# A two-layer graph network with experts: GpSimd adds half of the six expert answers to the other half, and TensorE sums the rest with 12 transposes, not 24

## The chip, the cores and the metric

The kernel runs on one core of a Trainium2 chip. The core has five engines that work side by side, each through its own list of instructions, in order: TensorE (PE in the profile, its weight loads PEld), VectorE (DVE), ScalarE (ACT), GpSimd (POOL) and SyncE (SP), which here only issues DMA transfers. TensorE writes to PSUM; the others work on SBUF, and VectorE and ScalarE read PSUM too. The metric is the device time of one execution in microseconds. Of three runs of the kernel before, the median is 2058.91 us (2055.96 to 2059.22).

## The reference

The input is 8192 tokens of 256 numbers (128 graphs of 64 nodes). There are two layers, each a graph step and an expert step. The part around the change is the end of layer 0 and the start of layer 1:

```python
# layer 0, experts: top 6 of 64, each a 256x256 matrix
xW = einsum('bsd,bskde->bske', x, lattice_weights[indices])   # six answers a token
lattice_out = einsum('bske,bsk->bse', xW, scores)             # their weighted sum
h = x + einsum('bsd,ed->bse', lattice_out, out_w) + out_b
x = x_in + layer_norm(h)                                      # x_in: the input of this step
# layer 1, graph step
h = layer_norm(x)
conv = (adj @ h) @ W_rel + b_rel + h @ W_root
x = x + relu(conv)
```

Then layer 1 routes every token to its top 2 of 8 experts with a hidden layer of 512 and adds their two answers. All of it is float32.

## The kernel before

The work is cut into 32 blocks of 256 tokens (two tiles of 128, `T = 2`). It runs in four stages. The first does layer 0's graph step and sends each token six times to a table in DRAM that is sorted by expert. The second walks that table in pages of 128 rows, multiplies each page by its expert's matrix, scales the rows by the token's score and scatters them to `r0.answer` in DRAM, so that the six answers of a token lie side by side. The third, called the fused pass here, is the one that the change touches. The fourth does layer 1's experts, again page by page.

The fused pass takes a block through these steps:

- `load_y` (L970) brings the block's answers into the tile `y`, 128 partitions x 2 tiles x 6 answers x 256 numbers, with two DMAs of 768 KB. For the first five blocks (`READY = 5`) it need not wait for the last answers, for the later ones it must.
- `load3` (L979) loads `xn1`, `x1` and the adjacency.
- `mixture` (L987) both sums the six answers and turns them: for each half of the 256 numbers and each tile, six matmuls with the identity, marked as transposes, are accumulated in PSUM (L994). That is 24 a block. ScalarE copies the result to `accT` (L997).
- `out_proj` (L999) is the product with `out_w`; `layer_out_h`, `_a`, `_b`, `_c` (L1008 to L1049) are the residual and both layer norms, mostly on VectorE (L1011, L1017, L1026, L1028 and the statistics of L45 and L46).
- `flip_h`, `neighbours`, `convolve_a`, `convolve_b` (L1051 to L1084) are layer 1's graph step on TensorE, and `residual1_a`, `residual1_b` (L1086, L1094) its residual and norm.
- `flip3` and `gate1` (L1102, L1108) compute the routing logits on TensorE; `choose1` (L1115) starts on VectorE with L1118, finds the two experts, and has GpSimd write the token numbers into `xs` (`compare`, L292); `count1` counts on TensorE (L217).
- `place1` and `send1` (L1129, L1136) work out each token's row on VectorE (L313 to L327, then L296) and send it with an indirect DMA from GpSimd (L334), four a block. `xs` has three buffers.

The loop is software-pipelined. `staggered` (L486) runs through steps; in step s, a stage with lag g works on block s - g. So `load_y` with lag -3 works three blocks ahead of `layer_out_h` with lag 0, and `mixture` with lag -2 two blocks ahead. Within a step the order is that of the list at L1143.

The order of instructions on TensorE, VectorE and ScalarE is this written order (`manual_schedule`, L515). On GpSimd and SyncE a planner sets the order at compile time: it plays the program through with estimated costs and takes, on each of these engines, what it believes to be ready first. On GpSimd, for instance, the `compare` of a block stands ahead of the last sends of the block before. Every engine then works through its list strictly in order; waits between engines and on DMAs are semaphores that the framework places. A tile name with `bufs=n` has n buffers in turn; the work pool of this pass gives two where nothing else is said, so `y` has two, and the load of a block's `y` waits for the `mixture` of two blocks before.

Of the kernel before, what the change touches and what calls it, by code (L numbers as in the profile page):

```python
# [9 lines left out]
F32 = mybir.dt.float32  # L10
# [6 lines left out]
ALU = mybir.AluOpType  # L17
AX = mybir.AxisListType
PSUM = bass.MemoryType.PSUM
P = 128  # L20
# [465 lines left out]
def staggered(n, stages, first=0):  # L486

    for s in range(first + min(lag for lag, _ in stages), n + max(lag for lag, _ in stages)):
        for lag, f in stages:
            if first <= s - lag < n:  # L490
                f(s - lag)
# [3 lines left out]
def two_layer_gnn_moe_kernel(ctx: ExitStack, tc: tile.TileContext, a: dict, out: bass.AP):  # L495
    nc = tc.nc
    x_in, adjT = a["x"], a["adjT"]
    N, D = x_in.shape
# [4 lines left out]
    T = 2  # L503
# [5 lines left out]
    K0 = 6  # L509
    E1, F1, _ = a["L1_ffn_W2"].shape  # L510
    EARLY = 12
    READY = 5
# [91 lines left out]
    with tc.tile_pool(name="c0", bufs=1) as c0, \  # L604
# [9 lines left out]
        blocks = [dict() for _ in range(NB)]  # L614
# [213 lines left out]
        n = free[0] // 16  # L828
# [118 lines left out]
    with tc.tile_pool(name="c3", bufs=1, reuse_waits="tile") as c3, \  # L947
# [17 lines left out]
        blocks = [dict() for _ in range(NB)]  # L965
# [3 lines left out]

        def load_y(b):  # L970
            B = blocks[b]
            B["y"] = y = work.tile([P, T, K0, D], F32, name="y")
            for t in range(T):
                d = nc.sync.dma_start(out=y[:, t],
                                      in_=r0.answer[ts(b * T + t, P * K0), :].rearrange("(p k) d -> p k d", k=K0))
                if b < READY:
                    tc.declare_no_dep(d.ins, group="r0last", reason="in the first pages, or waited for above")

        def load3(b):  # L979
            B = blocks[b]  # L980
            B["xn1"] = xn1 = work.tile([P, T, D], F32, name="xn1", bufs=3)
            nc.sync.dma_start(out=xn1, in_=by_tile(xn1_dram[b]))
            B["x1"] = x1 = work.tile([P, T, D], F32, name="x1", bufs=3)
            nc.sync.dma_start(out=x1, in_=by_tile(x1_dram[b]))
            B["at"] = load_adjacency(b)

        def mixture(b):  # L987

            B = blocks[b]
            pt = psum.tile([P, KD, C], F32, name="ps")  # L990
            for t in range(T):
                for k in range(KD):
                    for i in range(K0):
                        nc.tensor.matmul(pt[:, k, ts(t, P)], lhsT=B["y"][:, t, i, ts(k, P)], rhs=ident,  # L994
                                         start=(i == 0), stop=(i == K0 - 1), is_transpose=True)
            B["accT"] = accT = work.tile([P, KD, C], F32, name="accT")
            nc.scalar.copy(accT, pt)  # L997

# [137 lines left out]
        def send1(b, i):  # L1136
# [4 lines left out]
            r1.send(B["row"], B["xs"], b > NB // 2, (k,), (t,))  # L1141

        staggered(NB, (  # L1143
            (-3, load_y),
            (-2, load3),
            (0, layer_out_h),
            (3, choose1),
            (-2, mixture),
            (1, flip_h),
            (3, count1),  # L1150
            (2, residual1_a),
# [127 lines left out]
```

## Time and profile before

| what | value |
|---|---|
| median of three runs | 2058.91 us |
| the profiled execution, its own time | 2052.92 us |
| its span, first to last instruction | 2051.1 us |
| mean granted TensorE clock | 0.974 |
| busy: TensorE / its weight loads | 1923.0 us (94%) / 1678.1 us (82%) |
| busy: VectorE / ScalarE / GpSimd | 1200.0 (59%) / 1018.1 (50%) / 1162.0 us (57%) |
| the fused pass, about | 1131 to 1525 us of the span |
| L994, the transposes of the answers | 768, 94.7 us of TensorE busy |

The profile is one execution. Engine times are the union of its instructions' times, so an engine at 94% over the whole span can be full in one stage and wait in another; the shares must be read by stage. Rows of a timeline give the start, the length, the engine, the line of the kernel, the operation, what it writes and reads with their shapes, and in brackets how long the engine had stood idle before it and what ended that. Rows of a single line or tile give the shortest, median and longest duration in ns. The time of an indirect DMA on GpSimd is that of its issue, not of the transfer.

### The profile page before, as it was taken

To read this page: it belongs to the slowest core of one execution; us is meant where nothing else is said; L and a number is where in the kernel's file an instruction comes from. 1 tells how busy PE (TensorE), PEld (TensorE's weight loads), DVE (VectorE), ACT (ScalarE), POOL (GpSimd) and SP (SyncE) were. 2 spreads that over 40 slices of the span, in tenths; PEclk is the share of its full clock that TensorE was granted. 3 is DMA by queue.
4 is the path that set the end of the run, shared out by engine and by line. 5 is a ranking of instruction groups with operands and counts; after the bars stand their busy time and mean duration, and the time that the engine had idled before them with its cause. 6 is when DMAs were issued, how large, how long until landed. Compare 5 with 4: busy or idle time off the path is not lost. (4 is left out here: it accounts for less than half of the span.)

```text
span 2051.1 us, 37214 instructions
## 1 busy us (share of the span) xinstructions
PE 1923.0 (94%) x10516; PEld 1678.1 (82%) x10516; DVE 1200.0 (59%) x4205; ACT 1018.1 (50%) x2033; POOL 1162.0 (57%) x1134
## 2 busy tenths in 40 slices
PE   6999999999966989999999799999989999999996
PEld 5888888888865778888877688888868888888885
DVE  5899999999975333344333389999862222222221
ACT  4888888888851222222222266666643333333332
POOL 1377667677677777777777723333343444444443
PEclk9999999999977999999999899999989999999998
DMA  4244555544476988666665799888527766666664
GB/s 123 80 143 148 168 165 170 169 159 141 133 267 206 309 252 267 214 207 207 207 207 171 266 362 338 267 278 278 190 92 172 178 162 162 162 163 163 163 163 86
DMA packets 282561, 397.91 MB, mean 194 GB/s; under 512 B 56025, under 2 KB 236393, under 8 KB 282353
## 3 DMA queue, kind: packets, MB, share of 16 engines
q1 hardware_dynamic: 202880, 246.61, 40.2%
q0 software_dynamic: 64416, 136.14, 22.1%
q10 hardware_dynamic: 15056, 12.69, 1.9%
q8 instruction: 94, 1.54, 0.3%
q14 instruction: 115, 0.93, 0.2%
HBM read 222.84 MB, written 176.64 MB: 195 GB/s over the span
## 5 line engine op out<-in xcount | busy, mean ns | idle before, releaser
L334 POOL DMA_INDIRECT r0x<-xs,r0row x384 | 402.1, 1047 | 236.0 <-DVE lat L706 72.2
L341 POOL DMA_INDIRECT r0y<-px x404 | 393.3, 973 | 123.3 <-DMA r0y<-px 49.7
L918 PE MATMUL py<-lat,pxT 128*128 x1616 | 389.4, 384 | 18.7 <-ACT pxT L905 15.4
L351 POOL DMA_INDIRECT out_x<-py_s,px x138 | 214.6, 1555 | 293.8 <-DMA out_x<-py_s,px 125.9
L922 DVE TENSOR_SCALAR px<-py,px 128x256 f32<-128x256 f32 x404 | 177.0, 480 | 309.6 <-PE py L918 303.9
L918 PEld LDWEIGHTS py<-lat,pxT 128*128 128x128 f32 x1616 | 294.3, 192 | 59.3 <-ACT pxT L905 20.4
L905 ACT COPY pxT<-pt 128x512 f32<-128x512 f32 x202 | 117.9, 585 | 368.6 <-PE pt L903 252.7
L1217 ACT ACTIVATE phid<-ph,pw 128x256 f32<-128x256 f32 x276 | 130.6, 473 | 323.2 <-issue 213.9
L1215 PE MATMUL ph<-pxT,pw 128*128 128x256 f32 x1104 | 251.3, 381 | 0.7 <-ACT pxT L1206 0.7
L1235 PE MATMUL py<-fw,phid 128*128 (+1 forms) x1104 | 249.7, 379 | 0.0
L717 PE MATMUL ps<-lat 128*128 128x256 f32 x1024 | 238.5, 382 | 0.0
L1215 PEld LDWEIGHTS ph<-pxT,pw 128*128 128x128 f32 x1104 | 210.9, 191 | 30.0 <-ACT pxT L1206 1.1
L684 PE MATMUL ph<-lat 128*128 128x256 f32 x1024 | 232.2, 386 | 2.7 <-DVE lat L706 2.0
L1235 PEld LDWEIGHTS py<-fw,phid 128*128 128x128 f32 x1104 | 204.5, 190 | 25.0
L684 PEld LDWEIGHTS ph<-lat 128*128 128x128 f32 x1024 | 195.1, 193 | 29.4 <-issue 2.4
L334 POOL DMA_INDIRECT r1x<-xs,r1row x128 | 127.7, 998 | 160.9 <-DVE r1run L313 47.0
L717 PEld LDWEIGHTS ps<-lat 128*128 128x128 f32 x1024 | 193.8, 192 | 24.9
L1229 DVE TENSOR_SCALAR p<-p 128x2 f32<-128x2 f32 x69 | 12.8, 186 | 225.5 <-ACT p L1228 225.5
L1238 DVE TENSOR_TENSOR py_s<-py,pb 128x512 f32<-128x512 f32 x69 | 47.7, 692 | 154.9 <-PE py L1235 152.7
L903 PE MATMUL pt<-ident,px 128*128 128x128 f32 x808 | 125.3, 276 | 11.6 <-DMA px<-r0x 11.3
L903 PEld LDWEIGHTS pt<-ident,px 128*128 128x128 f32 x808 | 100.4, 142 | 37.7 <-DMA px<-r0x 8.9
L994 PE MATMUL ps<-ident,y 128*128 128x128 f32 x768 | 94.7, 281 | 16.1 <-DMA y<-r0y 16.1
(303 smaller groups left out, 2980.4 us busy)
## 6 DMA issues: line engine op xcount, KB each, us to landing
px<-r0x SPq DMA_DIRECT2D x404, 129.0 KB
y<-r0y SPq DMA_DIRECT2D x64, 768.0 KB
pw<-in_L_ffn_W1b SPq DMA_DIRECT2D x69, 514.0 KB
px<-r1x SPq DMA_DIRECT2D x69, 258.0 KB
x<-x SPq DMA_DIRECT2D x64, 256.0 KB
pb<-in_L_ffn_b SPq DMA_DIRECT2D x69, 128.0 KB
r0x<-r0filler ACTq DMA_DIRECT2D x64, 129.0 KB
lat<-in_x SPq DMA_DIRECT2D x32, 256.0 KB
```

The costliest lines, as they stand in the source:

```text
L334: i = self.nc.gpsimd.indirect_dma_start(out=self.table[:, :], out_offset=bass.IndirectOffsetOnAxis(ap=row[:, t, k:k + 1], axis=0), in_=xs[ ...
L341: d = self.nc.gpsimd.indirect_dma_start(out=self.answer[:, :], out_offset=bass.IndirectOffsetOnAxis(ap=x[:, self.D:self.D + 1].bitcast(I32 ...
L351: i, d = f"{self.name}add{i}", self.nc.gpsimd.indirect_dma_start(out=self.total[:, :], out_offset=bass.IndirectOffsetOnAxis(ap=x[:, self.D ...
L684: nc.tensor.matmul(ph[:, c, :], lhsT=w1[:, k, ts(2 * j + c, P)], rhs=B["aggT"][:, k, :], start=(k == 0), stop=(k == KD - 1))
L717: nc.tensor.matmul(B["po"][:, t, :], lhsT=B["hT"][:, c, ts(t, P)], rhs=w2[:, c, :], start=False, stop=(t == T - 1 and c == KH - 1))
L903: nc.tensor.transpose(pt[:, k, ts(q, P)], Q["px"][:, q, ts(k, P)], ident)
L905: nc.scalar.copy(xT[:, :, :n * P], pt[:, :, :n * P])
L918: nc.tensor.matmul(py[:, q, :], lhsT=xT[:, k, ts(q, P)], rhs=lat[:, ds(regs["e"][(2 * j + q) % 4], 1), k, :].rearrange("p o d -> p (o d)") ...
L922: nc.vector.tensor_scalar(px[:, q, :D], py[:, q, :], px[:, q, D + 1:D + 2], None, op0=ALU.mult)
L1215: nc.tensor.matmul(ph, lhsT=w[:, k * F1 + c * P:k * F1 + (c + 1) * P], rhs=Q["xT"][:, k, :], start=(k == 0), stop=(k == KD - 1))
L1217: nc.scalar.activation(hid[:, c, :], ph, AF.Relu, bias=w[:, KD * F1 + c:KD * F1 + c + 1], scale=1.0)
L1235: nc.tensor.matmul(py[:, t, :], lhsT=Q["hid"][:, c, ts(t, P)], rhs=fw2[:, ds(e, 1), c, :].rearrange("p o d -> p (o d)"), start=(c == 0), s ...
```

## The change

From block 6 on (`b > READY`), a new step `halve` has GpSimd add the last three answers of each token to the first three, in place in `y`: two adds a block, each 128 partitions x 768 float32. `mixture` then accumulates three transposes for each quarter, 12 a block. The first six blocks are summed as before, by 24. `halve` works three blocks ahead (lag -3, listed behind `mixture` of the block before it), so `load_y` moves from three to four blocks ahead, and `y` gets a third buffer: 12,288 bytes more in each partition of the pass's work pool.

```diff
         def load_y(b):
             B = blocks[b]
-            B["y"] = y = work.tile([P, T, K0, D], F32, name="y")
+            B["y"] = y = work.tile([P, T, K0, D], F32, name="y", bufs=3)
...
+        def halve(b):
+
+            B = blocks[b]
+            B["n"] = K0
+            if b > READY:
+                B["n"] = h = K0 // 2
+                y = B["y"]
+                for t in range(T):
+                    nc.gpsimd.tensor_tensor(y[:, t, :h], y[:, t, :h], y[:, t, h:], op=ALU.add)
...
             for t in range(T):
                 for k in range(KD):
-                    for i in range(K0):
+                    for i in range(B["n"]):
                         nc.tensor.matmul(pt[:, k, ts(t, P)], lhsT=B["y"][:, t, i, ts(k, P)], rhs=ident,
-                                         start=(i == 0), stop=(i == K0 - 1), is_transpose=True)
+                                         start=(i == 0), stop=(i == B["n"] - 1), is_transpose=True)
...
         staggered(NB, (
-            (-3, load_y),
+            (-4, load_y),
             (-2, load3),
             (0, layer_out_h),
             (3, choose1),
             (-2, mixture),
+            (-3, halve),
             (1, flip_h),
```

## The prediction

> **What bounds the kernel now.** I read the chain of waits first, cut to the fused pass (1131 to 1525 us of the span), because the change touches only that pass. Columns: start, us, what.
>
> ```profile
> 1305.31 0.92 PE pg L1112 x8
> 1306.23 2.67 PE ps L994 x24
> 1308.90 0.44 PE ps L76 x4
> ...
> 1316.35 0.92 PE pg L1112 x8
> 1317.28 2.67 PE ps L994 x24
> ```
>
> One block takes 1317.28 - 1306.23 = 11.05 us and the chain never leaves TensorE: the pass looks TensorE-bound, and the 24 transposes of L994 are 2.67 us of each block, 0.111 us apiece. Second, the busy time by stretch, one steady block and then one block after the last transposes of L994 were done (1474.9 us), so a block in which TensorE has none of them left.
>
> ```profile
> core 0: us, PE busy (x) PEld busy (x) DVE busy (x) ACT busy (x) POOL busy (x), PEclk, DMA share, GB/s
> 1305.05:1316.10 11.05, 11.05 (x76) 9.90 (x74) 10.03 (x47) 7.15 (x17) 4.17 (x5) 1.00 0.78 244
> 1483.30:1494.00 10.70, 8.95 (x51) 7.28 (x50) 9.89 (x46) 6.17 (x14) 3.82 (x6) 1.00 0.21 74
> ```
>
> TensorE is full in the first and VectorE is at 10.03 of 11.05. In the second TensorE is down to 8.95 us, and VectorE's work is what it was. Third, then, VectorE's timeline: the instruction that opens each block's routing (L1118), three blocks in a row.
>
> ```profile
> 1472.25 0.17 DVE L1118 TENSOR_TENSOR logits<-pg,r_L_ffn_bg 128x16 f32<-128x16 f32 x1 [0.23 <-PE pg L1112]
> ...
> 1483.29 0.17 DVE L1118 TENSOR_TENSOR logits<-pg,r_L_ffn_bg 128x16 f32<-128x16 f32 x1 [0.23 <-PE pg L1112]
> ...
> 1494.03 0.16 DVE L1118 TENSOR_TENSOR logits<-pg,r_L_ffn_bg 128x16 f32<-128x16 f32 x1
> ```
>
> With the transposes a block took 11.04 us, of which VectorE waited 0.23 for TensorE. Without all 24 of them it took 10.74, and VectorE waited for nothing. So 10.74 us is VectorE's own time for a block, and TensorE hides a second bound only 0.31 us below its own. This is the view that decides the case.
>
> Fourth, whether GpSimd and VectorE disturb each other. Two pairs, from the timeline and from the instructions of one tile:
>
> ```profile
> 1156.78 0.66 DVE L1017 TENSOR_TENSOR x<-x,r_L_ffn_ln_b 128x512 f32<-128x512 f32 x1
> 1156.87 1.41 POOL L341 DMA_INDIRECT r0y<-px  x1 [0.30 <-DMA r0y<-px]
> ```
> ```profile
> L334 POOL DMA_INDIRECT r1x<-xs,r1row x128: 958/970/1524, 1194.4 to 1531.3; - x128
> L327 DVE CAST r1row<-r1rowf x32: 169/382/391, 1193.3 to 1524.6; 128x4 int32<-128x4 f32 x32
> ```
>
> A Pool instruction that takes 0.97 us took 1.41 when a VectorE instruction with two inputs in SBUF was running: 0.44 more. In the other direction the small CAST of L327 takes 0.17 us alone and 0.38 beside a Pool DMA issue: at 1304.36 it ended at 1304.74, with the issue of 1303.80 (0.97 us). They do make each other wait, in both directions.
>
> **The change, part by part.** *TensorE.* 26 blocks (6 to 31) lose 12 transposes each: 12 x 0.111 = 1.33 us of a block, 34.7 us in all, if TensorE alone set the pace. It does not: the block falls from 11.05 to 10.74 and stops there, because VectorE is next. That is worth 0.31 us a block.
>
> *Pool.* 52 adds of 128x768 f32, two a block. No row shows such an add. Low end: Pool's fills, from 128x1 in 99 ns to 128x516 in 528, cost 0.83 ns an element, so 0.74 us. One pass that reads and writes is the AFFINE_SELECT, 128x128 in 282 ns: (282 - 99) / 128 = 1.43 ns an element, so 0.1 + 1.1 = 1.2 us. High end: that pass twice, 2.3 us. I take 1.8, the read-and-write pass plus a second read at the fills' pace (0.64), as the add reads two operands and writes one. [...] Pool itself has room: 4.17 us busy in a block, 7.8 with the adds.
>
> *What the adds do to VectorE.* This is the term that decides. About a third of VectorE's instructions in a block read two tiles in SBUF (L209, L296, L68, L1017, L1026, L1028, L323, L1042), and the two casts behave as L327 does. No row shows an add on Pool beside them. From both sides: nothing is lost (the DMA issues, which read only an index, leave L323 at its 0.19), or such an instruction waits until the add is over, as the cast waited for the issue. I take the second, because the add streams SBUF through all of its time and the cast's row, where Pool also keeps moving data, is the nearest. I laid two adds of 1.8 us into the block from 1305.37 to 1316.40. Example, behind the token-number instruction that ends at 1309.05: the first add ends at 1310.85, L296 waits for it from 1309.41 (1.44 us); the second runs from 1310.98 to 1312.78, and L1017, now due at 1311.98, waits 0.80; together 2.24. Behind each of the four sends it is 3.49, 2.21, 3.44, 2.79; over all starting points of the block 2.7, which I take, as the planner's place for the adds is not known. With 0.74 us the mean is 0.8, with 2.3 it is 3.7 and the worst place 4.5. A block then takes 10.74 + 2.7 = 13.44 us, 2.39 more than now. Of 26 blocks I count 25 (the first pair falls into the wait for the last answers, before 1186 us): +60 us. [...]
>
> *The wait that is added.* A block's transposes now wait for its two adds; behind them on TensorE stand flip_h, the counts and all the rest of the block. The adds are due a whole block earlier, so I cost it at nothing; the cover is one block (13 us). On Pool an add waits for its y tile; behind it stand the compare and four sends, which free xs (three buffers).
>
> *y one block earlier, a third buffer.* The same 64 loads. SP issues each right after the transposes three blocks before (0.8 to 1.5 us of SP time, as now); 0.78 of the DMA engines' time is used in a steady block, so nothing. At the start block 5's y waits for the last answers (issued 1179.65) and now stands before block 3's xn and x loads (1159.21, 1162.02 now). VectorE's L1011 of block 3, at 1181.32 now, may slip until that y has landed, 1185.86: 0 to 4.6 us. I take 2. Below nothing: block 6's y gets out some 3 us sooner, but TensorE waits for no y after 1185.86.
>
> **Sum.** +60 + 2 = +62 us. On the profiled execution (span 2051.1, time 2052.9) that makes 2114.9; the median of the three runs, 2058.9, lies 6.0 above it, and I forecast against the median: 2121.
>
> **The rivals.** *No blocking* (ends on the other side): the adds share SBUF without holding VectorE up. Then a block takes 10.74: -0.31 x 25 = -8 us, 2051. For it: L323 at its 0.19 beside a Pool issue. Against: L327 and L341. It decides where the loss is under 0.31 us a block. *Short or sheltered adds*: 0.74 us each, or a place where VectorE runs statistics (two gaps of 1.1 and 1.8 us without a two-input instruction): loss 0.8, block 11.54, +12 us; with half of the 1.8-us loss 12.1, +26 us: 2071 to 2085. *Pool late*: the adds stand where y has not landed (block 5's took 6.2 us from issue), and sends and compare wait behind them. The sends' landing released the compare at 1308.83, 2.8 us ahead of ScalarE's refill of xs at 1311.62; 6.2 - 2.8 = 3.4 us a block reach flip3. Alone 14.1 us a block, +77 us, 2136; on top of the blocking up to 2206. *The whole 1.33 us is gained*: 2024; only if VectorE could go below 10.74, which the block from 1483.29 denies.
>
> **How the numbers follow.** Forecast 0.61, short or sheltered 0.18, no blocking 0.11, Pool late 0.08, whole gain 0.02. The range, 2066 to 2165, runs from the sheltered adds to 2.3-us adds in the worst place (10.74 + 4.5 = 15.24, +105 us, 2164); it leaves out no blocking, the whole gain and half of Pool late, 0.17. A measurement of this kernel tells about 0.2% (4 us) from no change. Faster: most of no blocking and the whole gain, 0.11; same: the rest of it and the edge of the sheltered adds, 0.04; slower 0.85.
>
> **What would show it.** Right: L994 at 12 transposes and 1.3 us a block from block 6; TensorE no longer the whole chain of a block but waiting for VectorE; VectorE's L296, L68, L1017 or L1026 lengthened or started late beside a Pool TENSOR_TENSOR of some 1.8 us; L1118 13 to 14 us apart. Wrong: those rows at their old lengths and L1118 10.7 apart (no blocking), adds under 1 us, or TensorE or Pool waiting on y's DMA (Pool late).

## The result, and the profile after

The kernel after the change takes 2135.44 us (median, 2130.45 to 2141.96) against 2059.06 us of the kernel before, measured beside it: a ratio of 1.0376, with a 95% interval of 1.0339 to 1.0413. That is 76.4 us slower. The forecast was 2121 us, +62.

The profiled execution took 2141.96 us (span 2140.2), the slowest of its runs. The change adds ten lines ahead of the loop, so the line numbers of the pass move: L994 is now L1004, L1011 is L1021, L1017 is L1027, L1026 is L1036, L1028 is L1038 and L1118 is L1128. The adds are L987.

First, the busy time by stretch, as it was read before the change: two blocks with adds beside them, then one after the last add.

```profile
core 0: us, PE busy (x) PEld busy (x) DVE busy (x) ACT busy (x) POOL busy (x), PEclk, DMA share, GB/s
1388.23:1416.25 28.02, 22.65 (x131) 18.99 (x129) 26.50 (x94) 14.21 (x31) 15.70 (x15) 0.93 0.64 212
1553.86:1564.59 10.73, 10.00 (x61) 8.29 (x59) 9.93 (x48) 7.07 (x16) 4.21 (x6) 1.00 0.22 77
```

TensorE was full before (11.05 of 11.05 us in a steady block); now it works 22.65 of 28.02 us, and VectorE 26.50. With the adds over, a block takes 10.73 us, though it still has 12 transposes to do. The transposes by themselves, on TensorE's timeline, one row of before and two of after:

```profile
1383.41 2.82 PE L994 MATMUL ps<-ident,y 128*128 128x128 f32 x24
...
1386.55 2.80 PE L1004 MATMUL ps<-ident,y 128*128 128x128 f32 x12
...
1398.48 1.51 PE L1004 MATMUL ps<-ident,y 128*128 128x128 f32 x12
```

Twelve take 1.51 us where 24 took 2.82, so 1.31 us less. In five of the 26 blocks they take 2.80 us at a granted clock of 0.50 to 0.51; ahead of the one at 1386.55, TensorE had stood idle for 2.95 us until 1384.82. Second, VectorE's timeline, the instruction that opens each block's routing:

```profile
1359.19 0.16 DVE L1128 TENSOR_TENSOR logits<-pg,r_L_ffn_bg 128x16 f32<-128x16 f32 x1
1372.46 0.16 DVE L1128 TENSOR_TENSOR logits<-pg,r_L_ffn_bg 128x16 f32<-128x16 f32 x1
1388.23 0.16 DVE L1128 TENSOR_TENSOR logits<-pg,r_L_ffn_bg 128x16 f32<-128x16 f32 x1
1400.14 0.16 DVE L1128 TENSOR_TENSOR logits<-pg,r_L_ffn_bg 128x16 f32<-128x16 f32 x1
1416.25 0.16 DVE L1128 TENSOR_TENSOR logits<-pg,r_L_ffn_bg 128x16 f32<-128x16 f32 x1
...
1543.14 0.16 DVE L1128 TENSOR_TENSOR logits<-pg,r_L_ffn_bg 128x16 f32<-128x16 f32 x1
1553.86 0.16 DVE L1128 TENSOR_TENSOR logits<-pg,r_L_ffn_bg 128x16 f32<-128x16 f32 x1
1564.59 0.16 DVE L1128 TENSOR_TENSOR logits<-pg,r_L_ffn_bg 128x16 f32<-128x16 f32 x1
```

The steps are 13.27, 15.77, 11.91 and 16.11 us beside the adds and 10.72 after them, and the brackets are empty: at these openers VectorE waits for nobody (from 1200 to 1530 us it waits there 1.1 us in all for TensorE, in the profile of before 12.8). From the first opener to the last the pass takes 409.96 us, before it was 338.82: +71.1. From the first load of `y` to the first opener it is 56.34, before 51.80: +4.5. Together that is +75.7 us, as much as the medians differ by (76.4). The two profiled executions themselves lie 89.1 us apart; the other 13.4 us, 7.8 ahead of the pass and 5.6 behind it, lie in stages that the change does not touch.

Third, how the adds and VectorE's instructions stand to each other. The rows of single lines (shortest, median and longest ns):

```profile
L987 POOL TENSOR_TENSOR y<-y x52: 1795/1818/1893, 1197.5 to 1529.5; 128x768 f32<-128x768 f32 x52
L1027 DVE TENSOR_TENSOR x<-x,r_L_ffn_ln_b x32: 656/658/2747, 1166.6 to 1579.6; 128x512 f32<-128x512 f32 x32
L1036 DVE SCALAR_TENSOR_TENSOR h<-h,bn_mv,r_L_ffn_ln_g x64: 462/470/2758, 1168.9 to 1581.5; 128x256 f32<-128x256 f32 x64
L207 DVE CAST r1which<-r1idx x32: 169/170/1794, 1196.5 to 1606.4; 128x4 f32<-128x4 uint32 x32
```

An add takes 1.82 us. Instructions of 0.17 to 0.66 us become up to 1.8 to 2.8 us long. Three places of the timeline, from the two blocks above:

```profile
1395.99 1.81 POOL L987 TENSOR_TENSOR y<-y 128x768 f32<-128x768 f32 x1 [1.01 <-DMA y<-r0y]
1396.38 1.43 DVE L296 TENSOR_TENSOR xs<-r1top 128x1 f32<-128x1 f32 x1
...
1407.01 0.98 POOL L334 DMA_INDIRECT r1x<-xs,r1row  x1 [1.20 <-DMA y<-r0y]
1407.40 2.73 DVE L1036 SCALAR_TENSOR_TENSOR h<-h,bn_mv,r_L_ffn_ln_g 128x256 f32<-128x256 f32 x1
1408.02 1.82 POOL L987 TENSOR_TENSOR y<-y 128x768 f32<-128x768 f32 x1
...
1412.06 0.99 POOL L334 DMA_INDIRECT r1x<-xs,r1row  x1 [2.22 <-DVE r1run L313]
1412.61 2.32 DVE L327 CAST r1row<-r1rowf 128x4 int32<-128x4 f32 x1
1413.07 1.82 POOL L987 TENSOR_TENSOR y<-y 128x768 f32<-128x768 f32 x1
```

L296 (0.13 to 0.15 us as a rule) ends at 1397.81, 0.01 after its add. That is the forecast mechanism. The other two show more: L1036 starts 0.62 us ahead of the add's row, inside the row of the send, and still waits until the add is over, though those 0.62 us would have been enough for its 0.46. Its extra is 2.27 us for an add of 1.82. In the profile of before, the same instruction beside a send with no add behind it keeps its length:

```profile
1312.05 0.98 POOL L334 DMA_INDIRECT r1x<-xs,r1row  x1 [1.20 <-DVE h L1026]
1312.43 0.48 DVE L1026 SCALAR_TENSOR_TENSOR h<-h,bn_mv,r_L_ffn_ln_g 128x256 f32<-128x256 f32 x1
```

At the end of 50 of the 52 adds stands a lengthened VectorE instruction, and those are 78.3 us longer than their shortest in all. VectorE's busy time over the whole span grew by nearly as much, from 1200.0 to 1275.8 us. 31 adds stand directly behind a send (at most 0.15 us after its end) and hold VectorE up to 2.30 us; the other 21 never hold it longer than 1.62. GpSimd is little held up by the loads: the profile lists six waits of its adds for `y`, 8.6 us in all.

### The profile page after: what moved, and what is told of

Same layout as the page of the kernel before. It is cut to its first block, busy times and chain, and to the rows that moved or that the text cites. A ratio compares the mean times of both kernels' runs of the same rounds, so it can differ in the third digit from the quotient of the medians.

```text
span 2140.2 us, 36679 instructions
## 1 busy us (share of the span) xinstructions
PE 1934.9 (90%) x10204; PEld 1664.0 (78%) x10204; DVE 1275.8 (60%) x4205; ACT 1017.8 (48%) x2033; POOL 1263.6 (59%) x1186
## 5 line engine op out<-in xcount | busy, mean ns | idle before, releaser
L341 POOL DMA_INDIRECT r0y<-px x404 | 398.8, 987 | 123.1 <-DMA r0y<-px 46.0
L903 PE MATMUL pt<-ident,px 128*128 128x128 f32 x808 | 126.3, 276 | 13.9 <-DMA px<-r0x 13.5
L687 ACT ACTIVATE lat<-ph,c_L_gnn_b 128x256 f32<-128x256 f32 x256 | 103.4, 470 | 12.5 <-PE ph L684 10.6
```

The source lines that it names most:

```text
L341: d = self.nc.gpsimd.indirect_dma_start(out=self.answer[:, :], out_offset=bass.IndirectOffsetOnAxis(ap=x[:, self.D:self.D + 1].bitcast(I32 ...
L903: nc.tensor.transpose(pt[:, k, ts(q, P)], Q["px"][:, q, ts(k, P)], ident)
```

## The experiments

Of twelve runs, the first eight were taken where the stages ahead of the pass took longer (first routing opener at 1432 to 1481 us of the span, against 1183 to 1195 in the others; why is not known). The kernel before took 2336.65 us beside `e1` to `e4` and 2306.75 beside `e0`, `e5`, `e6` and `e8`; the last four stood against 2056.82. So ratios are compared, and "the pass", which is the time from the first routing opener to the last (338.82 us before, 409.96 after).

**The changed kernel again (`e0_after_again`).** No edit.

> The changed kernel once more, beside the runs of this call, since the chip of the first experiments ran the stages ahead of the pass some 280 us slower. Every theory: the pass, first to last routing opener, about 410 us against 339 before, blocks of 13 to 16 us, +71 to +77 us on whatever the kernel before takes here.

Ratio 1.0284 [1.0229, 1.0339], +68.6 us by the medians; the pass 404.60 us, a little under the expected 410. It is the yardstick for the first eight runs.

**No adds (`e1_no_adds`).**

```diff
-                for t in range(T):
-                    nc.gpsimd.tensor_tensor(y[:, t, :h], y[:, t, :h], y[:, t, h:], op=ALU.add)
```

> The two adds of a block are left out and nothing else: blocks 6 to 31 sum only the first three answers, by 12 transposes; the loads one block earlier and the third buffer stay. Theory (the adds hold VectorE up): VectorE sets the pace alone, the block falls from 14.2 us in the changed kernel to 10.72, the start stays 4.6 us late, so 11.05 - 10.72 = 0.33 us x 26 = 8.6 us gained against 4.6 lost: 2052 to 2058 us. Rival (the earlier loads, the third buffer or the new wait on TensorE cost the time): it stays near 2135. Rival (TensorE's 1.33 us a block is to be had once the adds are gone): 2025.

Ratio 0.9945 [0.9900, 0.9991], the pass 332.04 us. Two steps of VectorE's opener:

```profile
1618.63 0.17 DVE L1126 TENSOR_TENSOR logits<-pg,r_L_ffn_bg 128x16 f32<-128x16 f32 x1
1629.26 0.17 DVE L1126 TENSOR_TENSOR logits<-pg,r_L_ffn_bg 128x16 f32<-128x16 f32 x1
1640.00 0.17 DVE L1126 TENSOR_TENSOR logits<-pg,r_L_ffn_bg 128x16 f32<-128x16 f32 x1
```

With the adds gone and 12 transposes kept, a block is 10.7 us: 0.3 less than before, not 1.33. The adds cost 404.60 - 332.04 = 72.6 us. Against the changed kernel's first profile it is 409.96 - 332.04 = 77.9 us, and the lengthened VectorE rows counted there come to 78.3: they account for the whole cost. The transposes saved give back some 7 us in the pass (338.82 - 332.04; these two profiles are not of one time, but a block of the changed kernel without adds takes 10.72 us in both of its own). The rival in which the whole 1.33 us is gained falls.

**Adds, and all 24 transposes (`e2_adds_24`).** The last three answers of a token are counted twice in its sum here.

```diff
-                    for i in range(B["n"]):
+                    for i in range(K0):
```

> The adds stay on GpSimd, but TensorE goes on with all 24 transposes (so the last three answers count twice). Theory: VectorE is the bound with some 14 us a block, 24 transposes are hidden under it as 12 are, and the time is that of the changed kernel within 1%: 2120 to 2155 us. Rival (the halved transposes still save their 1.33 us a block in the changed kernel, and the adds cost all the more): 2165 to 2175.

Ratio 1.0239 [1.0196, 1.0281], the pass 388.42 us: not slower than the changed kernel (1.0284 in `e0`, so within the expected 1%), rather shorter. Twelve transposes more or less were worth nothing beside the adds here, where TensorE has room (in the changed kernel it works 22.65 of 28.02 us). That it came out 16 us shorter fits GpSimd's order, which the planner laid out otherwise: here 25 adds stand directly behind a send (33 in `e0_after_again`), and they hold VectorE 36.7 us in place of 60.8.

**One add a block (`e3_one_add`).**

```diff
-                for t in range(T):
-                    nc.gpsimd.tensor_tensor(y[:, t, :h], y[:, t, :h], y[:, t, h:], op=ALU.add)
+                nc.gpsimd.tensor_tensor(y[:, 0, :h], y[:, 0, :h], y[:, 0, h:], op=ALU.add)
```

> Only the first tile of a block is halved (one add a block, 6 + 12 transposes); the result is the same sum. Theory: half of the 3.3 us that VectorE loses in a block, 10.72 + 1.65 = 12.4 us, 1.3 us over the block of before x 26 + 4.6 at the start: 2090 to 2105. Rival (what costs is a queue or a start, not each add): near 2135. Rival (one add a block finds room between VectorE's instructions): under 2070.

Ratio 1.0104 [1.0065, 1.0143], the pass 362.96 us: 30.9 us above `e1_no_adds`, 43% of the 72.6 us of two adds, a little less than the half that was expected. The cost went about with the number of adds.

**Fills in place of the adds (`e4_fill`).** Three fills of the unused half, so that GpSimd is as busy, but only writes; those three answers are left out of the sum.

```diff
-                    nc.gpsimd.tensor_tensor(y[:, t, :h], y[:, t, :h], y[:, t, h:], op=ALU.add)
+                    for _ in range(3):
+                        nc.gpsimd.memset(y[:, t, h:], 0.0)
```

> In place of each add GpSimd fills the three answers that are not used any more, three times over (128x768 each, some 0.7 us, so 2.0 us for an add of 1.8; it waits for the same loads, writes as much, and reads nothing); the sum is that of three answers. Theory (an add holds VectorE up because it reads SBUF): VectorE's instructions with two SBUF inputs keep their lengths, only the small casts may wait; 10.7 to 11.3 us a block, 2052 to 2070. Rival (any GpSimd work in this place costs, by its queue, its sends or its writes): 2125 or more.

Ratio 1.0061 [1.0034, 1.0088], the pass 353.08 us, +21.0 over `e1_no_adds`, though the fills keep GpSimd longer (738 ns each, 2.2 us for three). That is at the upper end of what was expected, or just over it: many blocks lie at 11.7 to 12.6 us, not under 11.3. The rows of single lines of this kernel tell which instructions they reach:

```profile
L1037 DVE SCALAR_TENSOR_TENSOR h<-h,bn_mv,r_L_ffn_ln_g x64: 461/472/481, 1456.7 to 1810.4; 128x256 f32<-128x256 f32 x64
L1028 DVE TENSOR_TENSOR x<-x,r_L_ffn_ln_b x32: 656/659/660, 1453.5 to 1808.5; 128x512 f32<-128x512 f32 x32
L207 DVE CAST r1which<-r1idx x32: 170/251/1836, 1482.4 to 1835.5; 128x4 f32<-128x4 uint32 x32
L988 POOL MEMSET y<- x156: 728/738/767, 1471.3 to 1762.4; 128x768 f32 x156
```

The instructions of L1037 and L1028, with two SBUF operands, keep their lengths (481 and 660 ns at most, where the adds made them 2758 and 2747), though 21 of the 64 and 11 of the 32 ran beside a fill. L296, which has two as well, grows to 1.17 us, but there it starts 0.08 us behind a held cast of L327 and ends with it (1588.61 and 1588.53, both to 1589.78). The casts still stretch, to 1836; those of L207 are 16.3 us longer in all, most of the 21.0. So in these runs the adds, which read SBUF, hold the first kind, and the fills, which only write, don't; the casts of L207 are held by both (to 1794 ns beside the adds, to 1836 beside the fills). That it is the reading is a conclusion from these two kernels alone: an add and a fill differ in length too (1.82 and 0.74 us).

**The adds on VectorE (`e5_vector_adds`).**

```diff
-                    nc.gpsimd.tensor_tensor(y[:, t, :h], y[:, t, :h], y[:, t, h:], op=ALU.add)
+                    nc.vector.tensor_tensor(y[:, t, :h], y[:, t, :h], y[:, t, h:], op=ALU.add)
```

> The same two adds a block, on VectorE in place of GpSimd. An estimate: such an add reads two tiles in SBUF and is 768 numbers a partition; the addition of ln_b (two such operands, 512 numbers) takes 0.66 us, so about 0.95 us each and 1.9 us a block on VectorE. Theory (VectorE's queue is the bound, at 10.72 us, and GpSimd's adds cost it 3 us a block by locking SBUF): a block of 12.6 us, nothing lengthened beside GpSimd but what was so before, pass 339 + 25 x 1.57 + 4.5 = 383 us, +44 us, so faster than the changed kernel by some 30 us. Rival (what costs is the longer path from the load of y over an adding engine to the transposes, not the lock): as slow as the changed kernel or slower, +71 us or more, with TensorE waiting on the adds.

Ratio 1.0150 [1.0096, 1.0204], against 1.0284 of the changed kernel in `e0`: 29.5 us faster than it, by the medians. The pass is 377.11 us (383 expected).

```profile
1551.92 0.16 DVE L1128 TENSOR_TENSOR logits<-pg,r_L_ffn_bg 128x16 f32<-128x16 f32 x1
1553.26 1.82 DVE L987 TENSOR_TENSOR y<-y 128x768 f32<-128x768 f32 x2
1564.39 0.16 DVE L1128 TENSOR_TENSOR logits<-pg,r_L_ffn_bg 128x16 f32<-128x16 f32 x1
```

Two adds take 1.82 us on VectorE, as long as one takes on GpSimd, and a block is an even 12.47 us: 10.72 and 1.82, less 0.07. VectorE's queue sets the block, as the theory has it. The bound engine did the work itself and lost less than it lost to the engine that was to help it (the pass 377.11 us against 404.60 in `e0`).

**VectorE relieved of one instruction, with and without the adds (`e6_after_no_bias`, `e8_no_adds_no_bias`), and in the kernel before (`e7_before_no_bias`).** In each, the addition of ln_b (0.66 us) is left out; in `e8` the two adds are too.

```diff
-            nc.vector.tensor_add(B["x1"], B["x1"], ln_b.unsqueeze(1).to_broadcast([P, T, D]))
```

> The changed kernel without one VectorE instruction of 0.66 us with two operands in SBUF, the addition of ln_b to layer 0's norm (x + ln_b, left out; ln_b isn't added). Theory (VectorE's queue is the bound of a block): at least 0.6 us a block less over all 32, so 17 to 25 us less than the changed kernel, more where this instruction was one that waited behind an add. Rival (a block is bound by TensorE waiting for the adds, or by GpSimd's queue): within 5 us of the changed kernel.

> 12 transposes of three answers with no adds (the last three answers are left out of the sum), and without the addition of ln_b. Theory (without the adds VectorE's own 10.72 us is the floor, TensorE has 9.7 us of work): a block of 10.1 us, pass 339 - 25 x 0.95 + 4.5 = 320 us, 12 us less than the kernel without adds alone (332). Rival (something other than VectorE holds a block at 10.72 us): a block of 10.7 us again, pass 332 us.

> The kernel before without the addition of ln_b on VectorE (0.66 us; ln_b isn't added). Theory (before the change TensorE's queue is the bound of a block, 11.05 us, VectorE has 0.31 us to spare): blocks of 11.05 us as before, within 4 us of the kernel before, though VectorE has 0.5 us less to do. Rival (VectorE was the bound already): 10.6 us a block and 13 us less.

`e7`: ratio 1.0003 [0.9993, 1.0012]. Before the change these 0.66 us of VectorE are worth nothing, and the profile shows where it went:

```profile
1416.80 0.17 DVE L1117 TENSOR_TENSOR logits<-pg,r_L_ffn_bg 128x16 f32<-128x16 f32 x1 [0.68 <-PE pg L1111]
1427.84 0.17 DVE L1117 TENSOR_TENSOR logits<-pg,r_L_ffn_bg 128x16 f32<-128x16 f32 x1 [0.69 <-PE pg L1111]
```

Blocks of 11.04 us as before, and VectorE waits 0.68 us for TensorE in place of 0.23. `e8`: ratio 0.9885 [0.9839, 0.9932], blocks of 10.26 us, the pass 317.89 us, 14.2 less than `e1_no_adds`:

```profile
1608.40 0.16 DVE L1125 TENSOR_TENSOR logits<-pg,r_L_ffn_bg 128x16 f32<-128x16 f32 x1
1618.65 0.16 DVE L1125 TENSOR_TENSOR logits<-pg,r_L_ffn_bg 128x16 f32<-128x16 f32 x1
1628.91 0.16 DVE L1125 TENSOR_TENSOR logits<-pg,r_L_ffn_bg 128x16 f32<-128x16 f32 x1
```

With 12 transposes the same instruction takes 0.46 us off every block. TensorE was the bound before, VectorE is 0.3 us behind it, and is the bound from there. `e6`: ratio 1.0209 [1.0155, 1.0263], 16.4 us less than the changed kernel by the medians (17 to 25 expected) but only 9.9 us less in the pass (394.71). Its blocks after the last add are 10.26 us (10.72 in `e0`); its adds hold VectorE 74.6 us in the pass (73.5 in `e0`). The rival's "within 5 us" is out, but of the 14 us of 0.46 us a block, 4 did not show in the pass; why is open.

**Only the earlier loads and the third buffer (`e9_loads_only`).** The kernel before with the new lag and buffer, no adds, all 24 transposes.

```diff
-            B["y"] = y = work.tile([P, T, K0, D], F32, name="y")
+            B["y"] = y = work.tile([P, T, K0, D], F32, name="y", bufs=3)
...
-            (-3, load_y),
+            (-4, load_y),
```

> The kernel before with only the earlier load of y and the third buffer, and all 24 transposes: no adds. Theory: the blocks stay at 11.05 us, and the start of the pass loses 0 to 4.6 us, since block 5's answers now stand ahead of block 3's xn and x on SyncE's queue: 0 to +5 us. Rival (the third buffer lets the loads collide with the sends): blocks longer than 11.05 us.

Ratio 1.0009 [0.9998, 1.0020], +1.0 us by the medians. The start is as foreseen: from the first load of `y` to the first opener it takes 55.7 us (51.8 before). The waits of VectorE in that stretch, us in total, times, longest, show why:

```profile
DVE h L1018 <- DMA xn<-xn: 7.9, 2, 7.2
```

VectorE waits 7.2 us for block 3's `xn`, which block 5's answers now precede; in the kernel before the profile lists no wait for it. Of the 3.9 us lost, 2.1 come back in the first step of the pass, 10.58 us against 12.74 (the pass is 336.68 us, 338.82 before). The blocks stay at 11.05 us: the third buffer harms nothing.

**The adds' place on GpSimd (`e10_behind_compare`, `e11_behind_send`).** GpSimd's order is fixed by hand: in `e10` compare, add, add, four sends; in `e11` compare, two sends, add, add, two sends. Each instruction is bound behind the one before it:

```diff
+        def queue():
+            return tc.issue_after(r1.last.ins) if r1.last else nullcontext()
...
-                    nc.gpsimd.tensor_tensor(y[:, t, :h], y[:, t, :h], y[:, t, h:], op=ALU.add)
+                    with queue():
+                        r1.last = nc.gpsimd.tensor_tensor(y[:, t, :h], y[:, t, :h], y[:, t, h:], op=ALU.add)
```

> The changed kernel with GpSimd's order fixed in every step: compare, the two adds, then the four sends. First theory (an add holds up a VectorE instruction with two SBUF inputs while its own row of 1.82 us lasts): 2.24 us a block, as laid out in the prediction, block 12.98 us, no VectorE instruction lengthened by more than 1.85 us behind the first add. Second theory (only an add queued directly behind a send holds VectorE longer, from inside the send's row): the same here, since no add stands directly behind a send, 12.98 us. Both: pass about 339 + 25 x 1.93 + 4.5 = 392 us. Rival (the place makes no difference, the adds cost what they cost): 13.8 us a block, pass 410 us.

> The same two adds with GpSimd's order fixed as compare, send, send, the two adds, send, send, so that every first add stands directly behind a send whose landing nobody has to wait for. First theory (the add holds VectorE for its own row alone): 2.3 to 2.8 us a block, block 13.0 to 13.5 us, pass 393 to 408 us, no VectorE instruction lengthened by more than 1.85 us. Second theory (from inside the send's row on): L1036's product of h, which starts about 0.4 us into the send, is held until the add is over, up to 2.4 us, then the next instruction by the second add: up to 4.3 us, block up to 15 us, pass up to 445 us.

`e10`: ratio 1.0398 [1.0377, 1.0419], the pass 409.67 us, blocks of 13.88 us on the average from the second to the last with adds, ten of them 13.91 to 13.98. One of these from its timeline, with the openers at its two ends:

```profile
1345.90 0.17 DVE L1136 TENSOR_TENSOR logits<-pg,r_L_ffn_bg 128x16 f32<-128x16 f32 x1
1346.59 0.23 POOL L293 TENSOR_SCALAR xs<-r1dest 128x4 int32<-128x4 f32 x1
1346.90 3.56 POOL L995 TENSOR_TENSOR y<-y 128x768 f32<-128x768 f32 x2
1346.92 1.80 DVE L208 CAST r1which<-r1idx 128x4 f32<-128x4 uint32 x1
1348.76 1.75 DVE L210 TENSOR_TENSOR r1hot<-r1expert,r1which 128x32 bf16<-128x32 f32 x1
...
1359.82 0.17 DVE L1136 TENSOR_TENSOR logits<-pg,r_L_ffn_bg 128x16 f32<-128x16 f32 x1
```

The cast is held by the first add (1.63 us extra), the next instruction with two SBUF inputs by the second (1.56): 3.19 us, and 10.72 + 3.19 = 13.91 for a block of 13.92. In nine other blocks the cast is held only 1.07 to 1.22 us, and VectorE first waits 0.33 to 0.47 us for TensorE's logits; they take 13.79 to 14.18 us, since the cast ends with the first add wherever it starts, and the compare ahead of that add starts 0.07 us behind the last send of the block before. So the order fixed by hand also ties VectorE's block to GpSimd's queue. The expected 12.98 was wrong about the place: compare ran 0.7 us behind the opener (opener 1345.90), not 2.6 as in the profile of before (1306.27 and 1308.83), so the adds met the cast and not L296. The rival's 410 us was met for another reason than its own, as `e11` shows: ratio 1.0536 [1.0517, 1.0555], the pass 440.51 us, blocks of 14.8 to 15.3 us. Here one instruction carries all of the loss:

```profile
1404.91 0.98 POOL L335 DMA_INDIRECT r1x<-xs,r1row  x1 [1.20 <-DVE h L1044]
1405.30 4.48 DVE L1044 SCALAR_TENSOR_TENSOR h<-h,bn_mv,r_L_ffn_ln_g 128x256 f32<-128x256 f32 x1
1405.91 3.56 POOL L995 TENSOR_TENSOR y<-y 128x768 f32<-128x768 f32 x2
```

The product of h, 0.46 us by itself, starts 0.61 us ahead of the first add's row, inside the send's row, and waits through the send's end and both adds: 4.02 us extra, and so in 25 of the 26 blocks with adds (100.5 us). The first theory, a hold for the add's own row, gave 13.0 to 13.5 us a block and falls; the second gave up to 15, but had the second add hold the next instruction, not the same one. So the place of the same two adds is worth 30 us: 440.51 against 409.67 us of pass, 2167.75 against 2137.36 us of time.

In `e10` three casts were held through both adds (2.66 to 3.36 us extra), so the statement that no hold there passes 1.85 us was wrong three times: two adds back to back didn't always let VectorE in between them.

## Why the prediction was right

It said slower, by VectorE being held up beside the adds, and the time lies in its range. By its steps:

- *TensorE bound, VectorE's floor 0.31 us below.* Right. The floor was forecast at 10.74 us from one block; `e1` and the changed kernel's last blocks show 10.72, and `e7` and `e8` show the turn from one bound to the other. The whole gain of 1.33 us a block was never to be had. The transposes themselves saved 2.82 - 1.51 = 1.31 us where 12 x 0.111 = 1.33 was put; beside a floor set by VectorE this moved nothing.
- *An add of 1.8 us*, from the AFFINE_SELECT's row and the fills' pace: 1.82. The low end, 0.74, was that of a fill: 738 ns in `e4`.
- *2.7 us a block lost to the adds.* 78.3 us of lengthened rows are 3.0 us in each of 26 blocks; the 72.6 us between `e0` and `e1` are 2.8. The mechanism is right (rows of before had shown it only on a cast and on an issue), the size a little low. What the step lacked: it held VectorE for the add's row alone. Behind a send the hold begins inside the send's row, which is where the extras above 1.82 us, up to 2.30, come from; and 31 of 52 adds stood there. "Behind each of the four sends" was worked out at 2.21 to 3.49 us; the one tried cost 4.02. That the mean over all places came so near is in part luck: `e10` and `e11` lie 30 us apart by the place alone, and the planner's order was not known. The openers of the changed kernel are 11.6 to 16.1 us apart beside the adds, not an even 13 to 14.
- *25 blocks of 26.* The first pair was left out as hidden by the wait for the last answers. The whole pass gives 71.1 us, or 2.73 in each of 26 blocks, where 25 x 2.39 = 60 was put: 8.5 us for the size and 2.7 for the block left out.
- *The start, 0 to 4.6 us, 2 taken.* 4.5 in the changed kernel, 3.9 in `e9` (and 1.0 of its whole time). With this term the miss of 14 us, +62 for +76, is accounted for: 8.5 + 2.7 + 2.5.
- *No cost for the new wait of the transposes and for y's loads.* Right: TensorE has room (VectorE waited 1.1 us in all for its logits), GpSimd is listed with 8.6 us of waits for `y`, and the blocks of `e9` are unchanged. "Pool late" gave 2136 us, which is the time measured, by a cause that the profile denies: a forecast time that is met does not show its mechanism.

**No version here that sums all six answers beats the kernel before.** With VectorE's work as it is, the most that fewer transposes can bring is the 0.3 us a block of `e1`, which leaves three answers out. An add on VectorE costs 0.91 to 0.95 us there and saves half of 2.82 - 1.51 on TensorE, 0.66. With 0.33 us between the two engines' floors, one add in about five blocks would level them, an estimated 3 to 4 us in all. That is no more than the 4 us that the prediction put as the least that can be told from no change, and it wasn't tried.

## What to carry to other kernels

Before work is moved off a full engine, look for a stretch in which that engine lacks the work already: the next bound can be read there, and it caps the gain. GpSimd's adds, which read and write `y` in SBUF, were not free beside a VectorE that was nearly full (10.03 of 11.05 us): where they met an instruction with two SBUF inputs or a cast, they lengthened it, by 78.3 us for 52 adds, 1.5 us for each 1.82. As an estimate from these numbers, price such an instruction at first at about its own length again on VectorE, and compare that with doing the work on VectorE. The order on GpSimd is part of the price: the same two adds cost 30 us more directly behind a send than behind the compare (440.51 against 409.67 us of pass).

## What the runs showed of the hardware that was not expected

- An add that stood directly behind an indirect DMA issue on GpSimd held VectorE from inside the issue's row: up to 0.6 us ahead of the add's own (L1036 at 1407.40, L1044 at 1405.30). An issue alone didn't hold that instruction (0.48 us at 1312.43 in the profile of before). Why is not shown; no view here tells whether the add begins earlier than its row does.
- A VectorE instruction that had started to wait was passed by a second add whose row starts after its own (in 25 of 26 blocks of `e11`, 4.02 us extra, and in 3 of 26 of `e10`, 2.66 to 3.36).
- TensorE's granted clock was lower in the stretch with the adds: from 1200 to 1530 us it was 0.97 in the kernel before (busy 318.7 of 330 us) and 0.91 after (268.0 us), 0.84 in a block of `e11` (1399.12 to 1414.39, busy 12.23 of 15.27 us), and 1.00 again in the changed kernel's block from 1553.86, once the adds were over. Idle time alone doesn't tell it: in two blocks of `e5` (1551.92 to 1576.85) the clock was 1.00 with TensorE busy 21.30 of 24.93 us. Where it was 0.50, twelve transposes took as long as 24 before (2.80 us at 1386.55). Little was lost by it in the changed kernel, since VectorE set the pace (at its openers it waited 1.1 us in all for TensorE from 1200 to 1530 us).
